# Layer 0's gates made with tanh and dealt out over the slots, and the next image's context started later

## The chip, the cores and the metric

The kernel runs on one core of a Trainium2 chip. The metric is the device time of one execution in microseconds (us); the number given for a kernel is the median of its runs. For the kernel before, three runs took 9255.66, 9257.32 and 9263.38 us, so the median is 9257.32 us.

The engines are named as in the profile: PE multiplies matrices (PEld is its weight load, which runs beside it), DVE is the vector engine, ACT the scalar engine that evaluates functions such as exp, POOL the general engine, SP the engine whose queue issues most of the DMA transfers. Each engine works through its own instructions in order.

## What is computed

Two layers are applied to eight images of 128 x 128 pixels with 128 channels. The change lies in layer 0 and in one part of layer 1 that layer 0's loop computes in advance. Cut to what matters:

```python
# layer 0: linear attention, per image; x is (pixels, 128)
q, k, v = split(x @ w_qkv, 3)                  # 4 heads of 32 channels
q = softmax(q, over the 32 channels of a head) * 32 ** -0.5
k = softmax(k, over all pixels of the image)
context = k^T v                                # 32 x 32 per head
o = (q context) @ w_out + b_out
x1 = layernorm(o) * gamma + beta + x
# layer 1: a selective scan; of it only the gate concerns us
xz = x1 @ Win
xb, z = split(xz, 2)                           # 256 channels each
...                                            # convolution, four scans, their sum y
out = layernorm(y * silu(z)) @ Wout
```

Here silu(z) = z * sigmoid(z), which also equals (z/2) * (1 + tanh(z/2)).

## The kernel before, in words

`layer0` keeps two whole images in on-chip memory, `xs[0]` and `xs[1]`, each a tile of 128 channels (partitions) by W = 128 columns by H = 128 rows in float32. Images are taken in the order ORDER = (0, 1, 4, 5, 2, 3, 6, 7); "image 3" below means the fourth of them. An image is worked on in NG = 32 groups of 512 pixels (GW = 4 columns). Every matmul of layer 0 is float32, and the program issues each as two passes.

Two pipelines of stages run over the groups.

- The **context** of an image (function `context`): `key` multiplies group g with the key weights (tile pk, L180) and ACT copies it out (k, L182). `larger` keeps a running maximum on DVE (L190, L192, and every fourth group L196, L197). `fold` and `spread` turn it into a new bound every fourth group (L206 to L221). `value` makes the values (pv, L225; copied by ACT, L226). `subtract` (DVE, L231) and `raise_to` (ACT exp, L234) make the exponentials, and `add` multiplies them with the values into the sum pc (L240).
- The **attention** of an image (function `attend`): `query` makes pq (L268), its maximum qm (DVE, L270) and the difference q (DVE, L272). `exponent` is the exponential (ACT, L275). `normalize` sums it (qs, L280), inverts it (L281) and scales q on POOL (L282). `through_wo` makes pg (L288), which ACT copies to gt (L290). `through_context` makes po (L294), adds the bias into o (DVE, L296) and squares it (ACT sq, L298). `variance` reduces that (var, L302). `scale` makes the diagonal matrix d on POOL (L308 to L313). `turn` makes pt (L321), and `finish` scales it (ACT x1t, L325) and adds the input in place, on POOL (L327).

A third piece is the **gate** (`gate_group`, L147): silu of the second half of x1 @ Win, two matmuls pz per group (L161), ACT's Silu from PSUM into z (L163) and a store to the array zs in HBM (L165). For images 0 to 5 of the order, the group is first copied by DVE into a small tile v, from `xs` read across its columns (L152, a step of 512 bytes between elements). For images 0, 1, 4 and 5 that copy also goes to HBM as x1. Since v takes one row from every column, it can only be made once the whole image is finished.

What sets the order of the work: `in_order` ties every instruction to the one recorded ahead of it on the same engine, so that the order in which `image(b)` calls its stages is the order on each engine. `image(b)` runs the attention of image b and the context of image b + 1 side by side in slots t = 0 to 38 (LATER = 1 delays the context by one slot). In each slot the stages of different groups stand in a fixed sequence. After slot 0 of images 1 to 6, `gate(b - 1)` does all 32 gate groups of the previous image in one block, and then issues the load of image b + 1 into the buffer that has come free. In the last image the gates are dealt out: slots 0 to 31 hold one gate group of image 6 each, and slots 4 to 35 one of image 7.

Buffers: all results of PE but two share six PSUM banks (pool `l0p`, tag "ps"). The tiles z and k share seven buffers (tag "k"). The tile v has four.

Of the kernel before, what the change touches and what calls it, by code (L numbers as in the profile page):

```python
# [8 lines left out]
F32 = mybir.dt.float32  # L9
BF16 = mybir.dt.bfloat16  # L10
AF = mybir.ActivationFunctionType
ALU = mybir.AluOpType
# [4 lines left out]
P = 128  # L17
B = 8
# [3 lines left out]
NC2 = 2  # L22
R = 8
K = 4
GW = 4
GN = GW * H
NG = W // GW
BK = 4
ORDER = (0, 1, 4, 5, 2, 3, 6, 7)
LATER = 1  # L30
CH = 1024
CW = CH // H
NCH = L // CH
# [44 lines left out]
def layer0(ctx: ExitStack, tc, xT, w_qkv, w_out, b_out, gamma, beta, win, x1, zs):  # L78
# [12 lines left out]
    nc = tc.nc  # L91
    const = ctx.enter_context(tc.tile_pool(name="l0c", bufs=1))
    wp = ctx.enter_context(tc.tile_pool(name="l0w", bufs=2))
    sm = ctx.enter_context(tc.tile_pool(name="l0s", bufs=4))
    ps = ctx.enter_context(tc.tile_pool(name="l0p", bufs=6, space=PSUM))
# [10 lines left out]
    nc.sync.dma_start(wq, w_qkv)  # L106
    wz = const.tile([P, NC2 * P], F32, name="wz")
    nc.sync.dma_start(wz, win[:, NC2 * P :])
    wo = const.tile([P, P], F32, name="wo")
    nc.sync.dma_start(wo, w_out)  # L110
    bb = const.tile([P, GW, P], F32, name="bb")
# [13 lines left out]
    xs = [const.tile([P, W, H], F32, name=f"x{i}") for i in range(2)]  # L125
# [13 lines left out]
    def group(b, g):  # L139
        return xs[b % 2][:, g * GW : (g + 1) * GW, :]  # L140

    def load(b, pieces=range(8)):
        for i in pieces:
            s = slice(16 * i, 16 * i + 16)
            nc.sync.dma_start(xs[b % 2][:, s, :], xT[ORDER[b], :, s, :])

    def gate_group(b, g):  # L147

        v = group(b, g)
        if ORDER[b] % K < 2 or ORDER[b] < B // 2:  # L150
            t = wp.tile([P, GW, P], F32, name="v", bufs=4)
            nc.vector.tensor_copy(  # L152
                t, xs[b % 2].rearrange("p w h -> p h w")[:, g * GW : (g + 1) * GW, :]
            )
            if ORDER[b] < B // 2:
                nc.sync.dma_start(x1[ORDER[b]][:, g * GN : g * GN + GN], t.rearrange("p w h -> p (w h)"))
            if ORDER[b] % K < 2:
                v = t
        for c in range(NC2):
            pz = ps.tile([P, GW, P], F32, name="pz", tag="ps")  # L160
            nc.tensor.matmul(pz, wz[:, c * P : c * P + P], v, start=True, stop=True)  # L161
            z = wp.tile([P, GW, P], F32, name="z", tag="k", bufs=7)
            nc.scalar.activation(z, pz, AF.Silu)  # L163
            dst = zs[ORDER[b], c][:, g * GN : g * GN + GN]
            nc.sync.dma_start(dst, z.rearrange("p w h -> p (w h)"))  # L165

    def gate(b):

        for g in range(NG):
            gate_group(b, g)  # L170
        if b + 2 < B:
            load(b + 2)

    def context(b):

        ks, pks, ms, runs, scales = {}, {}, {}, {}, {}

        def key(g):
            pk = ps.tile([P, GW, P], F32, name="pk", tag="ps")
            nc.tensor.matmul(pk, wq[:, P : 2 * P], group(b, g), start=True, stop=True)  # L180
            ks[g] = k = wp.tile([P, GW, P], F32, name="k", tag="k", bufs=7)
            nc.scalar.copy(k, pk)  # L182
            pks[g] = pk

        def larger(g):
            pk = pks.pop(g)
            j, i = divmod(g, BK)
            if i == 1:
                runs[j] = run = wp.tile([P, GW, P], F32, name="run")
                nc.vector.tensor_tensor(run, pk, ks[g - 1], ALU.max)  # L190
            elif i > 1:
                nc.vector.tensor_tensor(runs[j], pk, runs[j], ALU.max)  # L192

            if i == BK - 1:
                run = runs[j]
                nc.vector.tensor_tensor(run[:, 0:2], run[:, 0:2], run[:, 2:4], ALU.max)  # L196
                nc.vector.tensor_tensor(run[:, 0], run[:, 0], run[:, 1], ALU.max)  # L197

        def fold(g):

            j, i = divmod(g, BK)
            if i < BK - 1:
                return
            run = runs.pop(j)
            turned = ps.tile([P, P], F32, name="pmt", tag="ps")
            nc.tensor.transpose(turned, run[:, 0, :], ident)  # L206
            ms[j] = m = sm.tile([P, 1], F32, name="m")
            nc.vector.tensor_reduce(m, turned, AX.X, ALU.max)
            if j:
                nc.vector.tensor_tensor(m, m, ms[j - 1], ALU.max)  # L210
                scales[j] = a = sm.tile([P, 1], F32, name="a")
                nc.vector.tensor_tensor(a, ms.pop(j - 1), m, ALU.subtract)
            runs[j] = dg = sm.tile([P, P], F32, name="dg", bufs=2)
            nc.vector.tensor_scalar(dg, ident, m, None, ALU.mult)

        def spread(g):
            j, i = divmod(g, BK)
            if i == BK - 1:
                nc.tensor.matmul(pm[:, j % 2, :], ones, runs.pop(j), start=True, stop=True)
                if j:  # L220
                    nc.scalar.activation(scales[j], scales[j], AF.Exp)  # L221

        def value(g):
            pv = ps.tile([P, GW, P], F32, name="pv", tag="ps")
            nc.tensor.matmul(pv, wq[:, 2 * P : 3 * P], group(b, g), start=True, stop=True)  # L225
            nc.scalar.copy(vts[g % 3][:, :, 0:P], pv)  # L226

        def subtract(g):

            mb = pm[:, g // BK % 2 : g // BK % 2 + 1, :]  # L230
            nc.vector.tensor_tensor(ks[g], ks[g], mb.to_broadcast([P, GW, P]), ALU.subtract)  # L231

        def raise_to(g):
            nc.scalar.activation(ks[g], ks[g], AF.Exp)  # L234

        def add(g):
            k = ks.pop(g)
            j, n = divmod(g, BK)
            for i in range(GW):
                nc.tensor.matmul(  # L240
                    pc, k[:, i, :], vts[g % 3][:, i, :],
                    start=(n == 0 and i == 0), stop=(n == BK - 1 and i == GW - 1),
                )
            if n < BK - 1:
                return
            if j:
                nc.vector.scalar_tensor_tensor(total, total, scales.pop(j), pc, ALU.mult, ALU.add)
            else:
                nc.vector.tensor_copy(total, pc)
            if g == NG - 1:  # L250
                rs = sm.tile([P, 1], F32, name="rs")
                nc.vector.reciprocal(rs, total[:, P : P + 1])
                for h in range(NH):
                    s = slice(HD * h, HD * h + HD)
                    nc.vector.tensor_scalar(
                        ctxs[b % 2][s, s], total[s, s], rs[s, :], HD**-0.5, ALU.mult, ALU.mult
                    )

        return key, larger, fold, spread, value, subtract, raise_to, add

    def attend(b):
# [69 lines left out]

        return query, exponent, normalize, through_wo, through_context, variance, scale, turn, finish

    def image(b):

        key = larger = fold = spread = value = subtract = raise_to = add = None
        query = exponent = normalize = through_wo = through_context = None
        variance = scale = turn = finish = None
        later = LATER if b >= 0 else 0
        if b + 1 < B:  # L340
            key, larger, fold, spread, value, subtract, raise_to, add = context(b + 1)
        if b >= 0:
            (query, exponent, normalize, through_wo, through_context, variance, scale, turn,
             finish) = attend(b)

        def at(stage, g):
            if stage is not None and 0 <= g < NG:
                stage(g)

        for t in range(later + NG + BK + 2):  # L350
            a = t - later
            at(scale, t - 2)
            at(finish, t - 3)
            at(query, t)
            if b == B - 1 and t < NG:
                gate_group(b - 1, t)
            at(through_wo, t - 1)
            if b == B - 1 and 4 <= t < NG + 4:
                gate_group(b, t - 4)
            at(exponent, t)  # L360
            at(subtract, a - BK - 1)
            at(raise_to, a - BK - 1)
            at(key, a)
            at(normalize, t)
            at(fold, a - 1)
            at(value, a - BK - 1)
            at(larger, a)
            at(through_context, t - 1)
            at(add, a - BK - 2)
            at(turn, t - 2)  # L370
            at(spread, a - 1)
            at(variance, t - 1)
            if t == 0 and 0 < b < B - 1:
                gate(b - 1)

    with in_order(tc):
        load(0)
        load(1)
        for b in range(-1, B):
            image(b)  # L380
# [889 lines left out]
```

## Time and profile before

| what | value |
|---|---|
| median of the three runs | 9257.32 us |
| the profiled execution, its own time | 9261.02 us |
| its span, first to last instruction | 9259.2 us |
| layer 0 (to about the first instruction of layer 1) | 0 to 2388 us |
| layer 1, front part, then scan part | 2388 to 4400, 4400 to 9259 us |

All readings are from the one profiled execution. Inside layer 0, the starts of the query's exponential (L275), of which there are 32 for each image, mark the images:

| stretch of the attention | starts at us | lasts us |
|---|---|---|
| context of image 0 alone | 0 | 112.7 |
| image 0 | 112.7 | 227.0 |
| image 1 | 339.7 | 297.8 |
| image 2 | 637.5 | 298.7 |
| image 3 | 936.2 | 288.2 |
| image 4 | 1224.4 | 286.0 |
| image 5 | 1510.4 | 296.5 |
| image 6 | 1806.9 | 296.2 |
| image 7 (the last) | 2103.1 | to 2388: 285 |

A line of a timeline gives the start in us, the length in us, the engine, the line of the kernel, the operation, what is written and read, and in brackets how long the engine had been idle before it and what it waited for. A line of groups gives the engine, the operation, its tiles and shapes and the count, then the busy time, the mean length of one in ns, and the idle time before them.

### The profile page before, as it was taken

The page shows a single profiled execution, that of the slowest core. Times are in us where ns is not written, and L with a number is a line of the kernel's source. Part 1 is how long each engine was busy: PE and PEld are TensorE (multiplying, and loading weights), DVE is VectorE, ACT ScalarE, POOL GpSimd, SP SyncE. Part 2 cuts the span into 40 slices and gives each one's busy share as a digit, 9 for nine tenths or more (in the row PEclk, how much of TensorE's full clock was granted, in tenths as well). Part 3 has the DMA queues.
Part 4 walks back from the last instruction along what each step waited for, and adds up shares of the span by engine and source line. Part 5 has one row for each costly group of instructions (what it writes and reads, how often), then busy time and mean ns, then how long its engine had stood idle before and what let it go on. Part 6 is the DMA issues. An engine that isn't in the chain of part 4 may idle for free. (4 is left out here: it accounts for less than half of the span.)

```text
span 9259.2 us, 91316 instructions
## 1 busy us (share of the span) xinstructions
PE 6337.5 (68%) x24512; PEld 3096.6 (33%) x24512; DVE 7992.0 (86%) x7953; ACT 7099.7 (77%) x8066; POOL 7316.5 (79%) x4684
## 2 busy tenths in 40 slices
PE   8899998988899999999434636446364463643636
PEld 5555555554333333333101304114031140311403
DVE  6667666774699999999799999999999999999996
ACT  5555555657789999999688887887878888888885
POOL 3446444554588988888599899998999989999897
PEclk9999999999999999999655757557575575755857
DMA  1322333123478789888758769587695876957767
GB/s 76 146 84 96 137 121 146 70 109 137 148 242 249 251 246 244 245 246 241 206 154 238 208 185 258 158 230 216 179 260 159 222 225 178 257 165 218 230 174 211
DMA packets 934769, 1750.66 MB, mean 189 GB/s; under 512 B 150228, under 2 KB 376148, under 8 KB 926064
## 3 DMA queue, kind: packets, MB, share of 16 engines
q1 hardware_dynamic: 873328, 1509.92, 49.4%
q0 software_dynamic: 60928, 234.90, 13.8%
q8 instruction: 200, 3.28, 0.1%
q14 instruction: 313, 2.56, 0.1%
HBM read 1052.36 MB, written 692.12 MB: 188 GB/s over the span
## 5 line engine op out<-in xcount | busy, mean ns | idle before, releaser
L951 POOL TENSOR_TENSOR h<-ubt,sp 128x1024 f32<-128x1024 f32 x1024 | 2422.4, 2399 | 348.4 <-ACT mv L1058 124.1
L934 PE MATMUL px<-rows,dtw 128*128 128x512 bf16 x2048 | 953.5, 565 | 2266.2 <-DVE y L1001 1084.5
L534 DVE SCALAR_TENSOR_TENSOR acc<-xb,cw,acc 128x1024 f32<-128x1024 f32 x1024 | 1320.3, 1289 | 133.7 <-ACT xb L502 89.9
L526 POOL TENSOR_TENSOR tap<-tap 128x1024 f32<-128x1024 f32 x512 | 1224.0, 2394 | 243.9 <-ACT tap L524 220.6
L938 ACT ACTIVATE sp<-px 128x1024 f32<-128x1024 f32 x1024 | 1047.3, 1024 | 435.4 <-PE px L934 418.1
L961 DVE TENSOR_TENSOR_SCAN h<-px,h 128x1024 f32<-128x1024 f32 x512 | 1177.3, 2331 | 31.7 <-ACT px L942 15.1
L934 PEld LDWEIGHTS <-dtw 128*128 128x128 bf16 x2048 | 169.1, 110 | 3089.1 <-issue 1022.7
L959 DVE TENSOR_TENSOR_SCAN h<-px,h 128x1024 f32<-128x1024 f32 x512 | 1177.9, 2330 | 21.4 <-POOL h L951 18.8
L1009 POOL TENSOR_TENSOR y<-y,h 128x512 f32<-128x512 f32 x768 | 1159.8, 1559 | 3.8 <-DVE h L982 3.8
L942 ACT ACTIVATE px<-sp,sa 128x1024 f32<-128x1024 f32 x1024 | 1110.4, 1109 | 6.1
L515 PE MATMUL acc<-xi,wt 128*128 128x512 f32 x2048 | 938.3, 601 | 53.7 <-ACT ures L539 53.7
L524 ACT ACTIVATE tap<-xb,cw 128x1024 f32<-128x1024 f32 x768 | 837.3, 1139 | 15.2 <-POOL xb L499 15.1
L282 POOL TENSOR_TENSOR q<-q,qs 128x512 f32<-128x512 f32 x256 | 272.2, 1063 | 695.5 <-DVE qs L281 695.5
L938 ACT ACT_TABLE_LOAD x512 | 656.9, 1283 | 170.0 <-PE px L934 168.0
L942 ACT ACT_TABLE_LOAD x512 | 656.9, 1283 | 9.1
L1074 PEld LDWEIGHTS px<-wg,z 128*128 128x128 f32 x4096 | 575.3, 225 | 114.8 <-issue 109.1
L1074 PE MATMUL px<-wg,z 128*128 128x128 f32 x4096 | 574.7, 308 | 0.0
L967 PE MATMUL pc<-rows,csel 128*128 128x512 bf16 x1024 | 517.5, 586 | 78.2 <-DVE rstd L1062 74.5
L515 PEld LDWEIGHTS acc<-xi,wt 128*128 128x128 f32 x2048 | 375.1, 189 | 574.4 <-issue 411.9
L488 PE MATMUL pxb<-xi,wi 128*128 128x512 f32 x1024 | 496.2, 607 | 2.1 <-ACT xb L497 2.1
L298 ACT ACTIVATE sq<-o 128x512 f32<-128x512 f32 x256 | 161.2, 630 | 421.0 <-DVE o L296 419.8
L1001 DVE TENSOR_TENSOR y<-y,px 128x1024 f32<-128x1024 f32 x384 | 468.6, 1220 | 14.4
(153 smaller groups left out, 15038.8 us busy)
## 6 DMA issues: line engine op xcount, KB each, us to landing
ubt<-ubs SPq DMA_DIRECT2D x1024, 512.0 KB
zs<-z SPq DMA_DIRECT2D x512, 256.0 KB
ubs<-ures SPq DMA_DIRECT2D x256, 512.0 KB
ubs<-turned SPq DMA_DIRECT2D x256, 512.0 KB
z<-zs SPq DMA_DIRECT2D x256, 512.0 KB
y<-gs POOLq DMA_DIRECT2D x128, 1024.0 KB, 10.3
gs<-du POOLq DMA_DIRECT2D x96, 1024.0 KB, 8.6
rows<-xps SPq DMA_DIRECT2D x1536, 60.0 KB
```

Source lines behind the costliest of these rows:

```text
L515: nc.tensor.matmul(acc[:, s, :], wt[:, j, c, :], x, start=(j == 0), stop=(j == len(ON_PE) - 1))
L524: nc.scalar.activation(t, at(n, c, *d), AF.Copy, scale=weight(n, c, *d))
L526: nc.gpsimd.tensor_tensor(sums[n, c], sums[n, c], t, ALU.add)
L534: nc.vector.scalar_tensor_tensor(acc, at(n, c, *d), weight(n, c, *d), acc, ALU.mult, ALU.add)
L934: nc.tensor.matmul(p[:, hf * 512 : hf * 512 + 512], sl.dw[:, c * P : c * P + P], src, start=True, stop=True)
L938: nc.scalar.activation(t, da[n, c], AF.Softplus)
L942: nc.scalar.activation(da[n, c], sp[n, c], AF.Exp, scale=sa[:, sl.s, c : c + 1])
L951: nc.gpsimd.tensor_tensor(h, u, t, ALU.mult)
L959: nc.vector.tensor_tensor_scan(e[:, ::-1], x[:, ::-1], e[:, ::-1], start, ALU.mult, ALU.add)
L961: nc.vector.tensor_tensor_scan(e, x, e, start, ALU.mult, ALU.add)
L1009: nc.gpsimd.tensor_tensor(v[:, c], v[:, c], h[:, c], ALU.add)
L1074: nc.tensor.matmul(po[:, w, :], z[:, c, w * H : w * H + H], wg[:, c, :], start=(c == 0), stop=(c == NC2 - 1))
```

## The change

1. **Gates with tanh.** The gate weights wz are halved once at the start. `gate_tanh` takes tanh of pz on ACT into z. `gate_store` makes (z + 1) * pz on DVE in one scalar_tensor_tensor and stores it. The bank pz is held until that is done.
2. **The copy v** (`ready`) moves from DVE to ACT, and is issued at the end of the slot ahead of the one whose gate uses it.
3. **The gates are dealt out.** `plan` gives every slot up to two gate groups. From slot 0 of image b, two groups of image b - 1 per slot until they are used up, and then the load of image b + 1. From slot 35, when the attention of image b is through, one group of image b itself per slot. The context of image b + 1 starts LEAD = 2 slots after the last gate of image b - 1. By these rules the contexts that run beside images 0 to 6 start at slot 1, 16, 9, 12, 11, 11 and 11 (`laters`), and these images have 39, 54, 47, 50, 49, 49 and 49 slots. The gates done in an image's own late slots are 4, 19, 12, 15, 14, 14 and 14. Image 7 has 37 slots: one gate in slots 0 to 4, two in slots 5 to 17, one from slot 18.
4. **Order inside a slot.** The exponential of the query (`exponent`) is now recorded ahead of `through_wo`, so ACT does it before the copy gt; it was the other way round. The gate's pieces stand between the stages as the diff shows.
5. **Buffers.** z has four of its own; k keeps seven.

```diff
--- before.py
+++ after.py
@@ -27,7 +27,7 @@
 NG = W // GW
 BK = 4
 ORDER = (0, 1, 4, 5, 2, 3, 6, 7)
-LATER = 1
+LEAD = 2
 CH = 1024
 CW = CH // H
 NCH = L // CH
@@ -106,6 +106,7 @@
     nc.sync.dma_start(wq, w_qkv)
     wz = const.tile([P, NC2 * P], F32, name="wz")
     nc.sync.dma_start(wz, win[:, NC2 * P :])
+    nc.vector.tensor_scalar(wz, wz, 0.5, None, ALU.mult)
     wo = const.tile([P, P], F32, name="wo")
     nc.sync.dma_start(wo, w_out)
     bb = const.tile([P, GW, P], F32, name="bb")
@@ -144,32 +145,35 @@
             s = slice(16 * i, 16 * i + 16)
             nc.sync.dma_start(xs[b % 2][:, s, :], xT[ORDER[b], :, s, :])
 
-    def gate_group(b, g):
+    vs, pzs, zts = {}, {}, {}
+
+    def ready(b, g):
 
         v = group(b, g)
         if ORDER[b] % K < 2 or ORDER[b] < B // 2:
             t = wp.tile([P, GW, P], F32, name="v", bufs=4)
-            nc.vector.tensor_copy(
-                t, xs[b % 2].rearrange("p w h -> p h w")[:, g * GW : (g + 1) * GW, :]
-            )
+            nc.scalar.copy(t, xs[b % 2].rearrange("p w h -> p h w")[:, g * GW : (g + 1) * GW, :])
             if ORDER[b] < B // 2:
                 nc.sync.dma_start(x1[ORDER[b]][:, g * GN : g * GN + GN], t.rearrange("p w h -> p (w h)"))
             if ORDER[b] % K < 2:
                 v = t
+        vs[b, g] = v
+
+    def gate_project(b, g):
+        v = vs.pop((b, g))
         for c in range(NC2):
-            pz = ps.tile([P, GW, P], F32, name="pz", tag="ps")
+            pzs[b, g, c] = pz = ps.tile([P, GW, P], F32, name="pz", tag="ps")
             nc.tensor.matmul(pz, wz[:, c * P : c * P + P], v, start=True, stop=True)
-            z = wp.tile([P, GW, P], F32, name="z", tag="k", bufs=7)
-            nc.scalar.activation(z, pz, AF.Silu)
-            dst = zs[ORDER[b], c][:, g * GN : g * GN + GN]
-            nc.sync.dma_start(dst, z.rearrange("p w h -> p (w h)"))
-
-    def gate(b):
-
-        for g in range(NG):
-            gate_group(b, g)
-        if b + 2 < B:
-            load(b + 2)
+
+    def gate_tanh(b, g, c):
+        zts[b, g, c] = z = wp.tile([P, GW, P], F32, name="z", bufs=4)
+        nc.scalar.activation(z, pzs[b, g, c], AF.Tanh)
+
+    def gate_store(b, g, c):
+
+        z = zts.pop((b, g, c))
+        nc.vector.scalar_tensor_tensor(z, z, 1.0, pzs.pop((b, g, c)), ALU.add, ALU.mult)
+        nc.sync.dma_start(zs[ORDER[b], c][:, g * GN : g * GN + GN], z.rearrange("p w h -> p (w h)"))
 
     def context(b):
 
@@ -178,7 +182,7 @@
         def key(g):
             pk = ps.tile([P, GW, P], F32, name="pk", tag="ps")
             nc.tensor.matmul(pk, wq[:, P : 2 * P], group(b, g), start=True, stop=True)
-            ks[g] = k = wp.tile([P, GW, P], F32, name="k", tag="k", bufs=7)
+            ks[g] = k = wp.tile([P, GW, P], F32, name="k", bufs=7)
             nc.scalar.copy(k, pk)
             pks[g] = pk
 
@@ -331,12 +335,36 @@
 
         return query, exponent, normalize, through_wo, through_context, variance, scale, turn, finish
 
+    plan, laters, loads = {}, {-1: 0}, {}
+    done = [0] * B
+    for b in range(-1, B):
+        left = NG - done[b - 1] if b > 0 else 0
+        if b >= 0:
+            laters[b] = -(-left // 2) + LEAD if left else 1
+        for t in range(laters[b] + NG + BK + 2 if b < B - 1 else NG + 5):
+            gates = plan[b, t] = []
+            for _ in range(2 if b < B - 1 else 1):
+                if b > 0 and done[b - 1] < NG:
+                    gates.append((b - 1, done[b - 1]))
+                    done[b - 1] += 1
+                    if done[b - 1] == NG and b + 1 < B:
+                        loads[b, t] = b + 1
+            if b < B - 1:
+                own = b >= 0 and not gates and t > NG + 2
+            else:
+                own = done[b] <= t - 5
+            if own and done[b] < NG:
+                gates.append((b, done[b]))
+                done[b] += 1
+    assert done == [NG] * B
+    times = list(plan)
+    then = dict(zip(times, times[1:]))
+
     def image(b):
 
         key = larger = fold = spread = value = subtract = raise_to = add = None
         query = exponent = normalize = through_wo = through_context = None
         variance = scale = turn = finish = None
-        later = LATER if b >= 0 else 0
         if b + 1 < B:
             key, larger, fold, spread, value, subtract, raise_to, add = context(b + 1)
         if b >= 0:
@@ -347,31 +375,46 @@
             if stage is not None and 0 <= g < NG:
                 stage(g)
 
-        for t in range(later + NG + BK + 2):
-            a = t - later
+        for t in (t for i, t in times if i == b):
+            a = t - laters[b]
+            first, second = (plan[b, t] + [None, None])[:2]
             at(scale, t - 2)
             at(finish, t - 3)
             at(query, t)
-            if b == B - 1 and t < NG:
-                gate_group(b - 1, t)
+            if first:
+                gate_project(*first)
+                gate_tanh(*first, 0)
+            at(exponent, t)
+            if first:
+                gate_tanh(*first, 1)
+                gate_store(*first, 0)
             at(through_wo, t - 1)
-            if b == B - 1 and 4 <= t < NG + 4:
-                gate_group(b, t - 4)
-            at(exponent, t)
+            if second:
+                gate_project(*second)
             at(subtract, a - BK - 1)
             at(raise_to, a - BK - 1)
             at(key, a)
             at(normalize, t)
+            if first:
+                gate_store(*first, 1)
+            if second:
+                for c in range(NC2):
+                    gate_tanh(*second, c)
             at(fold, a - 1)
             at(value, a - BK - 1)
             at(larger, a)
             at(through_context, t - 1)
+            if second:
+                for c in range(NC2):
+                    gate_store(*second, c)
             at(add, a - BK - 2)
             at(turn, t - 2)
             at(spread, a - 1)
             at(variance, t - 1)
-            if t == 0 and 0 < b < B - 1:
-                gate(b - 1)
+            for g in plan.get(then.get((b, t)), ()):
+                ready(*g)
+            if (b, t) in loads:
+                load(loads[b, t])
 
     with in_order(tc):
         load(0)
```

## The prediction

> **What bounds the kernel now.** I read the busy time by stretch first. Only layer 0, up to about 2388 us, is touched. Three stretches: one around the gate block after image 1's slot 0, one of attention beside context, one in the last image.
>
> ```profile
> core 0: us, PE busy (x) PEld busy (x) DVE busy (x) ACT busy (x) POOL busy (x), PEclk, DMA share, GB/s
> 339.00:407.00 68.00, 62.30 (x130) 24.03 (x131) 26.13 (x35) 40.16 (x66) 1.65 (x1) 0.95 0.90 341
> 407.00:637.00 230.00, 205.71 (x1047) 137.19 (x1045) 173.62 (x305) 131.15 (x231) 143.12 (x159) 0.98 0.12 46
> 2103.00:2388.00 285.00, 238.84 (x886) 126.27 (x884) 109.48 (x190) 224.19 (x318) 144.92 (x160) 0.98 0.38 144
> ```
>
> PE is the busiest everywhere, but pipelined matmuls overlap in the records, so I looked at one slot. This is the vector engine, from image 0:
>
> ```profile
> 258.14 0.68 DVE L270 TENSOR_REDUCE qm<-pq 128x16 f32<-128x512 f32 x1
> 258.93 0.69 DVE L272 TENSOR_TENSOR q<-pq,qm 128x512 f32<-128x512 f32 x1
> 259.53 0.68 DVE L231 TENSOR_TENSOR k<-k,pmx 128x512 f32<-128x512 f32 x1
> 260.31 0.69 DVE L280 TENSOR_REDUCE qs<-q 128x16 f32<-128x512 f32 x1
> ...
> 261.99 0.68 DVE L296 TENSOR_TENSOR o<-po,bb 128x512 f32<-128x512 f32 x1
> 263.43 0.69 DVE L302 TENSOR_REDUCE var<-sq 128x4 f32<-128x512 f32 x1 [0.76 <-ACT sq L298]
> ```
>
> q comes 5.88 us after q, and the chain that returns is DVE's own: q, wait for exp, qs, larger, o, wait for the square, var, qm, q. The two slots of four with extra maximum work take 7.4 and 7.0. So four slots take 26.2 us. The scalar engine in that slot has slack, and does gt ahead of the exponential, which waits for q:
>
> ```profile
> 258.80 0.59 ACT L290 COPY gt<-pg 128x512 f32<-128x512 f32 x1 [0.63 <-PE pg L288]
> 259.65 0.63 ACT L275 ACTIVATE q<-q 128x512 f32<-128x512 f32 x1 [0.27 <-DVE q L272]
> 260.25 0.63 ACT L234 ACTIVATE k<-k 128x512 f32<-128x512 f32 x1
> ...
> 262.76 0.63 ACT L298 ACTIVATE sq<-o 128x512 f32<-128x512 f32 x1 [0.93 <-DVE o L296]
> ```
>
> The last image repeats every 8.69 us, with two table loads in the chain from square to exp:
>
> ```profile
> 2222.22 0.63 ACT L298 ACTIVATE sq<-o 128x512 f32<-128x512 f32 x1 [1.58 <-DVE o L296]
> 2222.76 0.76 ACT L325 ACTIVATE x1t<-pt,gb 128x512 f32<-128x512 f32 x1
> 2223.54 1.28 ACT L163 ACT_TABLE_LOAD   x1
> 2224.84 1.08 ACT L163 ACTIVATE z<-pz 128x512 f32<-128x512 f32 x2
> ...
> 2227.41 1.28 ACT L275 ACT_TABLE_LOAD   x1
> 2228.70 0.63 ACT L275 ACTIVATE q<-q 128x512 f32<-128x512 f32 x1
> ```
>
> From the groups of the whole layer and the waits:
>
> ```profile
> PE pk L180 <- DMA x<-in_x: 67.4, 7, 15.4
> ```
>
> is the wait for the next image after each block (about 52 us without the first). For a copy like the one that moves to ACT, layer 1 has a row: 512 floats read with a step of 512 bytes.
>
> ```profile
> L606 ACT COPY turned<-ures x92: 1066/1087/1109, 2675.0 to 4393.2; 128x512 f32<-128x512 f32 x92
> ```
>
> **What the Trainium skill says.** "ScalarE: Activation LUTs", section "Table sets: the hidden batching unit": exp and tanh are in one set, so between them nothing is reloaded; no run here shows it yet, but the built program of the change has one load in layer 0, where the trace has 78. The same page, "What ACT_TABLE_LOAD costs", gives 1283 ns and as much again for a drain; the trace has 1283 ns, but the next function starts 1.30 us after the load's start, so I take 1.3. "Advanced Engine Details and Errata", "SBUF Cachelines": a read that meets a new 16-byte line with each element is penalised. The trace agrees: 1.09 us for the strided ACT copy against 0.57 to 0.63 for contiguous ones, and 0.77 for the DVE copy v.
>
> **The change part by part.** Pitches (start to start in a queue) from the timelines: a 512-column product on PE 0.86 to 0.89, end 1.02 after start, about 0.1 more after a wait; ACT 0.54 for exp and square, 0.47 to 0.49 from PSUM, 0.67 for x1t, 1.0 for the strided copy (1.09 to its end); DVE 0.61. (z + 1) * pz is not in the trace; the form of L534, 1289 ns for 1024, gives 0.69 for 512, bounded by 0.6 and 0.8. Tanh like Silu: 0.60, and it cannot gain, as the length is per element. Only closed chains count, because each engine is bound to its order.
>
> Attention beside context (A+C). The exponential now stands ahead of gt on ACT. gt feeds po, PE stands still at po, and the next pq is behind po, pc and pt. New chain: q 0.72, exp 0.54, gt 0.59, po 1.01, pc and pt 1.78, pq 1.02, qm 0.77 = 6.45 against 5.88. The 7.4 and 7.0 slots keep their own chain. Four slots: 27.3 instead of 26.2, so 6.83 a slot. The first five slots of a context lack pv and pc: 30.5 as before.
>
> Attention with two gates (A+2G). The two copies v stand behind the square on ACT, and the first gate product waits for the first copy, with pg, the second gate and po behind it on PE. Chain: o to sq 0.77, sq 0.54, copy 1.09, wait 0.05, five PE products 4.44, po 1.06 = 7.95. PE alone would need 6.95.
>
> Context with one gate (C+G). Closed through the copy again: copy 1.09, pz 1.10, tanh 0.63, store 0.64, subtract 0.69, raise 0.57, key and value copies 0.94 = 5.66; without the key copy, at the end, 5.2. PE alone: 4.45 and 3.5.
>
> Image with context delay L (images 1 to 6), from first exponential to the next image's: two starting slots 13.1; A+2G 7.95 (L-5); out of it 7.4; two slots of attention alone at 5.88; 30.5; 6.83 (26-L); from the last exponential over finish, POOL (17.2 in image 0 of the trace) and the copy to the first own gate 17.3; 5.66 (L-3); 5 x 5.2; last slot with the next query 5.9. Sum 232.8 + 6.78 L. The six L add up to 70, so 1871. Less 19, because image 6 needs no copies for its own gates, and 4 for two slots with only one gate: 1848. These images take 1763.4 now (2103.1 - 339.7): **+85 us**. In this the block (64 us each), the load waits (the load now has two slots of attention and more, some 13 us, against 8 us of waiting) and 12 table loads are gone.
>
> Image 0: 26 A+C slots at +0.28 are +7, four own gates at the end +12: **+19**.
>
> Image 7: no copies, no loads. One gate: exp, tanh, gt, po, o, sq, var, qm, q = 6.37. Two gates: PE, 7.05. 30 + 13 x 7.05 + 13 x 6.37 = 204.5 for the 31 steps that take 264.7 now: **-60**.
>
> Halving wz once costs under 0.5 us beside loads: nothing. The table load of layer 1's first Silu stays ahead of work that waits for DMA: nothing. Stores: four z buffers and four z in a slot. SP issues them in order behind the x1 store, which waits for POOL. I count their landing some 1 to 2 us ahead of the next tanh: nothing; if that cover is gone, about 1 us in 30 slots, +30. The x1 stores of the copies v go with them, 0.5 MB per slot of two, behind the z stores on SP; nothing near waits for them, as four tiles v last two slots.
>
> Sum: +85 + 19 - 60 = +44 on 9261.0 (the profiled run; span 9259.2) is 9305. The median is 3.7 lower: **9301**.
>
> **Rivals.**
> - *Engines' sums, not chains, set the slots* (faster). Then A+2G takes 7.05, C+G 4.55 and 3.6, A+C stays at 6.54: about -38, -93 and -38 from my sum, so 9132; half of it gives 9217. For it: PE is busiest in every stretch. Against it: the slot shown follows a chain and not PE's sum. It decides once A+2G falls below about 7.4 and C+G below 5.1.
> - *The copy on ACT costs what it costs on DVE*, 0.77: some 115 copies on the chain at -0.32 are -37, so 9264, no change. Layer 1's copies run while POOL reads the same tile, which may lengthen them; but they hardly vary (1066 to 1109).
> - *z stores come late* behind the x1 store: 9330.
> - *Tanh reloads tables after all*: excluded by the built program.
>
> **How the numbers follow.** A measurement can tell about 0.2% (18.5 us) from no change. Forecast 0.52 (own range 9276 to 9365: copy 1.0 to 1.1, DVE store 0.6 to 0.8, the handing over of each image within 5 us), late stores 0.08, cheap copy 0.13, engines' sums wholly or in part 0.27 (9130 to 9238). Slower 0.60, same 0.13, faster 0.27. The range runs from 9190, which leaves out about half of the last, to 9365.
>
> **What would show it.** In the profile after: v on ACT near 1.09 us and PE waiting at pz for it; exponentials 7.9 us apart in A+2G, 6.4 in plain A+C slots, 6.4 and 7.05 in image 7; gates in late slots every 5.7 us; no DMA wait before pk; layer 0 ending near 2432. I am wrong if v takes under 0.8 us, or if ACT isn't what PE waits for in slots with copies.

## The result, and the profile after

| kernel | median us | lowest to highest | ratio to before, 95% interval |
|---|---|---|---|
| before (6 runs) | 9256.99 | 9252.85 to 9264.19 | |
| changed (6 runs) | 9287.68 | 9281.18 to 9289.37 | 1.0032 [1.0021, 1.0043] |

The change makes the kernel slower by 30.7 us, or 0.3%. The forecast was 9301, so 44 slower, with a range of 9190 to 9365. The profiled execution of the changed kernel took 9287.93 us (span 9286.1). The busy times by stretch, for image 1, image 4 and the last image:

```profile
core 0: us, PE busy (x) PEld busy (x) DVE busy (x) ACT busy (x) POOL busy (x), PEclk, DMA share, GB/s
360.00:705.00 345.00, 297.22 (x1240) 174.47 (x1239) 225.46 (x403) 225.59 (x372) 144.20 (x160) 0.99 0.35 133
...
1316.00:1607.00 291.00, 263.88 (x1175) 159.98 (x1174) 207.35 (x370) 191.26 (x324) 143.88 (x160) 0.99 0.26 99
...
2179.00:2401.00 222.00, 200.44 (x834) 119.08 (x832) 170.69 (x289) 129.79 (x225) 143.69 (x160) 1.00 0.39 150
```

Image 1 now takes 344 us instead of 298, and PE stands idle for 48 of them. The last image takes 222 instead of 285: ACT's busy time there fell from 224 to 130. Layer 1's first instruction comes at 2401.5 us instead of 2388.2.

**A slot of attention beside context.** First ACT, then PE, then two lines of DVE, in image 0:

```profile
259.51 0.63 ACT L279 ACTIVATE q<-q 128x512 f32<-128x512 f32 x1 [1.38 <-DVE q L276]
260.05 0.57 ACT L294 COPY gt<-pg 128x512 f32<-128x512 f32 x1
...
266.00 0.63 ACT L279 ACTIVATE q<-q 128x512 f32<-128x512 f32 x1 [1.54 <-DVE q L276]
```

```profile
260.67 1.13 PE L298 MATMUL po<-gt,ctxn 128*128 128x512 f32 x2 [0.38 <-ACT gt L294]
261.63 1.05 PE L244 MATMUL pc<-vt,k 128*128 128x129 f32 x8
262.52 1.06 PE L325 MATMUL pt<-d,o 128*128 128x128 f32 x8
263.42 1.02 PE L272 MATMUL pq<-x,wq 128*128 128x512 f32 x2
```

```profile
264.48 0.69 DVE L274 TENSOR_REDUCE qm<-pq 128x16 f32<-128x512 f32 x1
265.27 0.69 DVE L276 TENSOR_TENSOR q<-pq,qm 128x512 f32<-128x512 f32 x1
```

Follow the times: exponential at 259.51, gt from 260.05 to 260.62, po at 260.67, pq at 263.42 to 264.44. On DVE qm then starts at 264.48 and q at 265.27, and the next exponential at 266.00. That is 6.49 us, and at no step is there more than about 0.1 us to spare. Before, ACT did gt first and the slot took 5.88.

**A slot of attention with two gates**, in image 1, PE and ACT:

```profile
395.43 1.98 PE L166 MATMUL pz<-v,wz 128*128 128x512 f32 x4 [0.71 <-ACT v L155]
397.25 1.05 PE L292 MATMUL pg<-wo,q 128*128 128x128 f32 x8
398.14 1.88 PE L166 MATMUL pz<-v,wz 128*128 128x512 f32 x4
399.86 1.02 PE L298 MATMUL po<-gt,ctxn 128*128 128x512 f32 x2
```

```profile
393.79 0.63 ACT L302 ACTIVATE sq<-o 128x512 f32<-128x512 f32 x1 [1.04 <-DVE o L300]
394.32 2.02 ACT L155 COPY v<-x 128x512 f32<-128x512 f32 x2
...
401.70 0.63 ACT L302 ACTIVATE sq<-o 128x512 f32<-128x512 f32 x1 [1.05 <-DVE o L300]
```

From square to square it is 7.91 us. In between, the first copy v ends near 395.4, PE starts the gate's products only then, and po, which leads to the next square, stands behind five products: four of the gates and pg.

**A late slot with one gate**, in image 1, ACT:

```profile
631.10 1.05 ACT L155 COPY v<-x 128x512 f32<-128x512 f32 x1
633.37 0.60 ACT L170 ACTIVATE z<-pz 128x512 f32<-128x512 f32 x1 [1.22 <-PE pz L166]
634.22 0.60 ACT L170 ACTIVATE z<-pz 128x512 f32<-128x512 f32 x1 [0.26 <-PE pz L166]
635.31 0.63 ACT L238 ACTIVATE k<-k 128x512 f32<-128x512 f32 x1 [0.49 <-DVE k L235]
635.85 0.57 ACT L186 COPY k<-pk 128x512 f32<-128x512 f32 x1
636.31 0.59 ACT L230 COPY vt<-pv 128x512 f32<-128x512 f32 x1
636.79 1.07 ACT L155 COPY v<-x 128x512 f32<-128x512 f32 x1
```

The copies are 5.7 us apart. ACT idles in this loop, and PE waits 1.1 us for v in each of the next slots; neither is full.

The last image has no table load any more. ACT in one of its one-gate slots, 6.37 us long:

```profile
2366.61 0.63 ACT L302 ACTIVATE sq<-o 128x512 f32<-128x512 f32 x1 [2.00 <-DVE o L300]
2367.15 0.76 ACT L329 ACTIVATE x1t<-pt,gb 128x512 f32<-128x512 f32 x1
2368.44 0.60 ACT L170 ACTIVATE z<-pz 128x512 f32<-128x512 f32 x1 [0.53 <-PE pz L166]
2369.39 0.63 ACT L279 ACTIVATE q<-q 128x512 f32<-128x512 f32 x1 [0.35 <-DVE q L276]
...
2372.98 0.63 ACT L302 ACTIVATE sq<-o 128x512 f32<-128x512 f32 x1 [2.00 <-DVE o L300]
```

Two more readings of layer 0: the waits for DMA (us in all, times, longest), and the row of the copy v (count, then shortest, median and longest in ns).

```profile
PE pk L184 <- DMA x<-in_x: 15.2, 1, 15.2
ACT z L170 <- DMA zs<-z: 6.7, 7, 1.8
```

```profile
L155 ACT COPY v<-x x192: 1042/1070/1121, 337.6 to 1947.2; 128x512 f32<-128x512 f32 x192
```

Only the first load is still waited for, and ACT waits less than 7 us for the four z buffers.

### The profile page after: what moved, and what is told of

It reads as the page before. It is cut to its first block, busy times and chain, and to the rows that moved or that the text cites. A ratio compares the mean times of both kernels' runs of the same rounds, so it can differ in the third digit from the quotient of the medians.

```text
span 9286.1 us, 92164 instructions
## 1 busy us (share of the span) xinstructions
PE 6287.3 (68%) x24350; PEld 3090.5 (33%) x24512; DVE 8120.8 (87%) x8274; ACT 7153.9 (77%) x8182; POOL 7313.0 (79%) x4684
## 5 line engine op out<-in xcount | busy, mean ns | idle before, releaser
L977 PE MATMUL px<-rows,dtw 128*128 128x512 bf16 x1893 | 911.7, 574 | 2307.8 <-DVE y L1044 1057.7
L175 DVE SCALAR_TENSOR_TENSOR z<-z,pz 128x512 f32<-128x512 f32 x512 | 343.0, 683 | 227.4 <-ACT z L170 226.9
L312 POOL TENSOR_SCALAR var<-var 128x4 f32<-128x4 f32 x256 | 49.4, 193 | 561.7 <-DVE var L306 561.7
```

The source lines that it names most:

```text
L977: nc.tensor.matmul(p[:, hf * 512 : hf * 512 + 512], sl.dw[:, c * P : c * P + P], src, start=True, stop=True)
```

## The experiments

Each ratio is to runs of the kernel before on the same chip. "Changed" stands for the kernel after the change, 9287.7 us.

| kernel | median us | ratio to before, 95% interval | start of layer 1 |
|---|---|---|---|
| e1, gt first | 9215.9 | 0.9954 [0.9941, 0.9966] | 2336.0 |
| e2, copies early | 9220.6 | 0.9957 [0.9945, 0.9970] | 2337.4 |
| e3, both | 9124.7 | 0.9852 [0.9837, 0.9867] | 2239.5 |
| e4, tanh in the block | 9629.6 | 1.0399 [1.0385, 1.0413] | 2752.0 |
| e5, the same, copy ahead | 9231.2 | 0.9974 [0.9963, 0.9984] | 2349.6 |
| e6, both, lead 1 | 9112.1 | 0.9844 [0.9830, 0.9857] | 2230.7 |
| e7, product without copy | 9200.0 | 0.9939 [0.9927, 0.9952] | 2314.1 |
| e8, Silu dealt out | 9627.1 | 1.0399 [1.0383, 1.0414] | 2755.1 |
| e9, both, lead 0 | 9140.8 | 0.9875 [0.9859, 0.9892] | 2260.2 |

### e1: gt first again

```diff
             at(query, t)
             if first:
                 gate_project(*first)
                 gate_tanh(*first, 0)
+            at(through_wo, t - 1)
             at(exponent, t)
...
-            at(through_wo, t - 1)
```

> The changed kernel with one order put back: in each slot ACT copies gt ahead of the query's exponential. Theory (closed chains through the order on ACT and PE): the 112 slots of attention beside context after the first five go from four slots in 27.15 us to 26.2, about -28 us, and the 16 one-gate slots of image 7 from 6.37 to about 5.9, -8: 9252 us. Rival (the swap is harmless, because ACT has idle time and the slot is set by sums of engine time): no change, 9288.

Measured: 9215.9, so 72 less than the changed kernel, twice the forecast. The slots went where they were expected, from 6.48, 6.48, 7.20, 6.99 to 5.89, 5.89, 7.39, 6.99. The rest came from slots that I had not counted: slots of attention alone fell from 5.88 to about 5.08, the first slots of each context from 5.88 to 5.65, in image 1 the slot after the last one with gates from 7.25 to 5.09, and the two-gate slots of images 5 and 6 from 7.22 to 7.00. Those of images 1 to 4 stayed (7.92 and 7.97): their chain over the copy is another one. One-gate slots of image 7 only fell to 6.21. The swap alone costs more than the whole loss of the change, so the rival is out.

### e2: the copies earlier in the slot

```diff
                 gate_store(*first, 0)
             at(through_wo, t - 1)
+            for g in plan.get(then.get((b, t)), ()):
+                ready(*g)
...
             at(variance, t - 1)
-            for g in plan.get(then.get((b, t)), ()):
-                ready(*g)
```

> The changed kernel with the strided copies v, the same in number and length and still on ACT, issued earlier in the slot: after the first gate's pieces and the copy gt, ahead of the exponential of the keys and of the square. Theory (the copy closes a chain over the gate's product on PE): two-gate slots of images 1 to 4 fall from 7.9 to about 7.0 (some 32 slots, -30 us), the late slots with one gate from 5.66 and 5.2 to about 4.5 and 3.5 (some 50, -64): 9193 us. Rival (the 192 x 1.07 us of ACT time are the cost, wherever they stand): no change, 9288. Rival (ACT is now late for the square or the keys): slower than 9288.

Measured: 9220.6, so 67 less, not 95. ACT's work is the same, so its amount is not what these 67 us were lost to. From the last exponential of image 1 to the next image it is 100 us instead of 124, as the late slots got shorter. But the two-gate slots stopped at 7.42, and those of images 5 and 6 rose from 7.22 to 7.42. ACT in such a slot of image 1:

```profile
392.59 0.63 ACT L279 ACTIVATE q<-q 128x512 f32<-128x512 f32 x1 [1.18 <-DVE q L276]
393.13 0.58 ACT L170 ACTIVATE z<-pz 128x512 f32<-128x512 f32 x1
393.60 0.58 ACT L294 COPY gt<-pg 128x512 f32<-128x512 f32 x1
394.07 2.11 ACT L155 COPY v<-x 128x512 f32<-128x512 f32 x2
396.09 1.07 ACT L170 ACTIVATE z<-pz 128x512 f32<-128x512 f32 x2
397.05 0.63 ACT L302 ACTIVATE sq<-o 128x512 f32<-128x512 f32 x1
...
400.02 0.63 ACT L279 ACTIVATE q<-q 128x512 f32<-128x512 f32 x1 [1.18 <-DVE q L276]
```

This is a new chain: exponential, tanh, gt, two copies, two tanh, square, and from there over DVE's var, qm and q to the next exponential at 400.02. ACT has no gap up to the square. The second rival was wrong for the sum, but it named this: ACT is now late for the square, and the slots of images 5 and 6 got longer.

### e3: both

Both edits together; `through_wo` stands ahead of `exponent`, and the copies follow the first gate's pieces.

> Both of the above edits in the changed kernel. Theory: the two chains lie in different slots, so the gains add: -36 and -95, about 9157 us, faster than both kernels. Rival (one stall hides the other): no better than the better of the two alone.

Measured: 9124.7, which is 163 below the changed kernel, more than the two alone added (72 + 67). Two-gate slots now come down to PE's sum, as e1 takes gt out of e2's new chain. PE in image 1:

```profile
401.58 1.02 PE L298 MATMUL po<-gt,ctxn 128*128 128x512 f32 x2
402.43 1.10 PE L325 MATMUL pt<-d,o 128*128 128x128 f32 x8
403.37 1.02 PE L272 MATMUL pq<-x,wq 128*128 128x512 f32 x2
404.23 1.88 PE L166 MATMUL pz<-v,wz 128*128 128x512 f32 x4
405.94 1.05 PE L292 MATMUL pg<-wo,q 128*128 128x128 f32 x8
406.83 1.88 PE L166 MATMUL pz<-v,wz 128*128 128x512 f32 x4
```

No brackets, no idle time: 6.95 us a slot. The chain over ACT and DVE, from one exponential (401.25) to the next (408.21), takes 6.96, so by the trace PE is not the only limit left. This kernel is faster than both others, by 1.5% than the one before.

### e4 and e5: tanh in the block

e4 is the kernel before with this alone (the diff is cut to the lines that matter):

```diff
+    nc.vector.tensor_scalar(wz, wz, 0.5, None, ALU.mult)
...
-            nc.scalar.activation(z, pz, AF.Silu)
+            nc.scalar.activation(z, pz, AF.Tanh)
+            nc.vector.scalar_tensor_tensor(z, z, 1.0, pz, ALU.add, ALU.mult)
```

> The kernel before with tanh alone: wz halved, tanh on ACT, (z + 1) * pz on DVE, everything else (gates in a block after slot 0, copy v on DVE, context one slot behind) as before. Theory (the tanh is the gain and the dealing out is the loss): image 7 falls from 8.7 us a slot to PE's sum of about 7.0, -49 us; twelve table loads at the six blocks are -15; the blocks gain nothing more, or lose up to 30 us in all, as DVE then has 2.0 us of work for each group beside 2.05 for the group: 9195 to 9225 us. Rival (the table loads were hidden): no change, 9257.

Measured: 9629.6, slower by 4%. Image 7 did fall to 6.94 a slot, but the first four blocks, whose products read v, took 171 to 174 us instead of 63 to 70. PE in such a block:

```profile
399.77 3.54 PE L162 MATMUL pz<-v,wz 128*128 128x512 f32 x4 [2.05 <-DVE v L153]
405.36 2.84 PE L162 MATMUL pz<-v,wz 128*128 128x512 f32 x4 [2.05 <-DVE v L153]
```

The next copy v stands on DVE behind this group's multiplications, which wait for tanh, which waits for the product, which waits for v. I had added up DVE's work and overlooked that it had become a closed chain of 5.4 us a group. PE is slow in it, too: the two products, 1.9 us in the dealt-out slots, take 2.7 to 3.6 us here, at a granted clock of 0.64 (345 to 505 us). e5 tests the reading by recording the next group's copy ahead (again cut):

```diff
+        if b < B - 2 and g + 1 < NG:
+            gate_copy(b, g + 1)
         for c in range(NC2):
```

> The kernel before with tanh in the block, as in the last run but with the copy v of the next group issued on DVE ahead of this group's two multiplications. Theory (the block of the last run closed a chain: v, product, tanh, multiplication, next v): the four blocks of images whose gates read v fall from 171 to 174 us back to 62 to 67, image 7 stays at 6.94 us a slot, and the twelve loads at the blocks are gone: 9190 to 9210 us, faster than before. Rival (tanh with its multiplication is too much for DVE in a block): blocks of 100 us and more, above 9400.

Measured: 9231.2. The chain is gone (blocks of 71 to 72 us, at a clock of 1.00 from 345 to 405 us), so the reading holds and the rival is out. These four blocks are not shorter than with Silu, and DVE has about 2.1 us of work per group in them: 0.73 for the copy and twice 0.69. I had expected 62 to 67, so the 9190 to 9210 were missed. Tanh with the gates left in their blocks is worth 0.3%. The last image gives more than that (230 us instead of 285); images 3 and 4 give some 19 us back.

### e6 and e9: how far the context must lag

Both have e3's orders; LEAD is 1 in e6 and 0 in e9.

> The changed kernel with both orders mended, and the next image's context one slot instead of two behind the last gate. Theory (a slot of lead costs 5.1 for a slot of attention alone and 4.2 for a late slot, against 6.5 for one of both): -2.7 us for each of six images, 9109 us against 9125, if the load still lands in time; it has then about 9 us. Rival (the load is late, as it was before the change): a wait for DMA ahead of pk of 3 us and more in each image, 9125 or slower.

> Both orders mended and no lead: the next context starts in the slot after the last gate of the image whose buffer it takes. Theory (the load needs about 9 us from its issue to the first piece, and only some 3 are left): pk waits for DMA about 5 us in each of six images, which more than eats the 2.7 us saved per slot: about 9125 us against 9112 with a lead of one. Rival (the load lands in time): 9100 or less.

Measured: 9112.1 and 9140.8. The waits of PE for the load, the first image left out, are these in e6 and then in e9:

```profile
PE pk L184 <- DMA x<-in_x: 1.1, 2, 0.6
```

```profile
PE pk L184 <- DMA x<-in_x: 28.0, 6, 5.2
```

So one slot of lead is enough and none is not: six waits of up to 5.2 us. e6's interval overlaps e3's, but its layer 0 ends 9 us earlier; its median is the lowest here. Both sizes were off. e6 gained 12.6 us on e3 and not 16. e9 came out 16 us above its forecast: the waits (28 us in all) are about those expected, but the second slot of lead saved next to nothing beside them, as layer 0 ends 29.5 us later than in e6. The load is also quicker than I had it: in e9 5.1 to 5.6 us pass from its issue on SP to the first product of the keys, and not 9, but that product is due within 1.4 us of the issue.

### e7: the product does not read the copy

```diff
-            if ORDER[b] % K < 2:
-                v = t
```

> The changed kernel with all copies v still made on ACT in the same place and stored to x1, but the gate products read the image's columns instead of v. This leaves out the turn of the gates of images 0, 1, 2 and 3, so zs holds their pixels in another order. Theory (the dependence of the product on the copy is the cost, not the copy's time on ACT): two-gate slots of images 1 to 4 fall from 7.93 to the 7.22 of images 5 and 6 (-22 us), and the late slots as in images 4 and 5 (78.7 us instead of 101.3 from the last exponential on in image 3), about -72 in all: 9194 us. Rival (ACT's time is the cost): 9288.

Measured: 9200.0, against 9194 expected. All 192 copies are still made, in the same places; only the gates' products do not wait for them. Two-gate slots fell from 7.92 to 7.22, and the stretch after the last exponential of image 1 from 124 to 101 us. In the changed kernel's order the dependence of the product on the copy costs 88 us; the same copies, when no product waits for them, are not what sets these slots. In e2's order their 2 us did stand in a chain, so this holds for the order and not for copies as such.

### e8: dealt out with Silu

The changed kernel without the halving of wz, with AF.Silu for AF.Tanh and without the multiplication in `gate_store`.

> The changed kernel with Silu in place of tanh: wz not halved, no multiplication on DVE, the gates dealt out in the same places. Its program has 364 table loads in layer 0. Theory (a load costs its 1.3 us only where ACT is on the chain: in two-gate slots and in image 7, and is hidden behind the wait for DVE and PE in the late slots): about 2 us in 47 two-gate slots, 2.3 in the 31 slots of image 7, 1 in the 92 late slots, about +260 on 9287: 9450 to 9600 us. Rival (all 363 added loads count): 9287 + 470 = 9757. Rival (ACT has room for them): 9287.

Measured: 9627.1, so 339 more for 363 loads, 0.93 us a load: above the 9450 to 9600 I gave, below the first rival's 9757. Two-gate slots of images 1 to 4 took 10.0 us as expected. But in late slots only half of the loads' time was hidden: from the last exponential of image 3 on it is 120 us instead of 101, so 1.3 us for each of 15 slots with two loads. And one-gate slots of image 7 took 10.24 us instead of 6.37, which is 3.87 more, while their two loads are 2.57. Most of the rest is po, in the changed kernel and then in e8:

```profile
2371.03 1.13 PE L298 MATMUL po<-gt,ctxn 128*128 128x512 f32 x2 [0.88 <-ACT gt L294]
```

```profile
2724.00 2.07 PE L297 MATMUL po<-gt,ctxn 128*128 128x512 f32 x2 [3.31 <-ACT gt L293]
```

The loads keep gt back, PE waits 3.3 us instead of 0.9, and po then takes 0.94 us longer. The granted clock in these slots is 0.83 (2660 to 2740 us), against 1.00 in the changed kernel's (2310 to 2390). So with Silu the gates dealt out in this order cost 4% against the kernel before. The Trainium skill's page "ScalarE: Activation LUTs", section "Table sets: the hidden batching unit", puts exp and tanh in one set, and the traces agree: one load in layer 0 with tanh, 364 with Silu.

## Why the prediction was right, step by step

In the profiled executions, from attention start to attention start, in us:

| image | forecast against before | measured |
|---|---|---|
| 0 | +19 | 248.1 - 227.1 = +21.0 |
| 1 to 3, by the forecast's formula | 341, 292, 314 | 344.2, 295.7, 315.5 |
| 4 to 6, by the formula | 305, 307, 288 | 291.3, 287.1, 284.9 |
| 1 to 6 | +85 | +55 |
| 7, to layer 1 | -60 | 222.0 - 285.1 = -63 |
| layer 0 | +44 | +13.3 |

**The chains held.** Attention beside context: 6.45 forecast (its terms as printed add up to 6.43), 6.48 measured. Two gates with a copy: 7.95 and 7.92. Late slots: 5.66 and 5.7. Image 7: 6.37 and 7.05, against 6.37 and 6.94. e1 and e2 opened the chains by order alone, e7 opened one by its data; this is shown, not only argued. The copy's price, 1.09 taken from layer 1, was 1.07.

**One term was mis-sized.** I let the copies of all of images 0 to 5 close the chain. For images 4 and 5 the copy only goes to x1 and the product reads the columns, so the late slots of these images, and the two-gate slots that do their gates (images 5 and 6), were overpriced: images 4, 5 and 6 came out 14, 20 and 3 us under the formula. The late part of images 4 and 5 took 78.7 us where that of image 3, with one slot more, took 101.3, and the two-gate slots of images 5 and 6 took 7.22 instead of 7.92. Against this, the first five slots of a context took 32.3 us in image 1 and 30.9 in images 2 to 6 where I had 30.5, as the swap on ACT costs there as well (in e1, which undoes it, they take 29.4), and the slot after the last one with gates took 7.25 us in most images instead of 5.88.

**Two things were not in the sum.** Layer 0 accounts for only 13 of the 27 us between the two profiled executions. By the first Silu of layer 1 the difference is 19.4. At the hand-over the last multiplication of the gates on DVE takes 5.75 us, behind a cast and beside POOL, which clears layer 1's buffers:

```profile
2403.13 5.89 DVE L464 CAST ident<-ident 128x128 bf16<-128x128 f32 x1
2403.27 5.75 DVE L175 SCALAR_TENSOR_TENSOR z<-z,pz 128x512 f32<-128x512 f32 x1
2403.89 4.43 POOL L496 MEMSET xb<- 128x5200 f32 x1
```

The last z store waits for it, and the first loads of layer 1 are queued behind that store on SP. From layer 1's start to its first Silu it is 31.0 us before and 37.2 here, and 36.2 to 37.4 in the other six kernels with tanh dealt out; but 32.0 and 32.2 in e5 and e4, where the last multiplication is over before POOL's long memset, and 30.8 in e8, which has none. So about 5 of the 6 us go with that multiplication, and about 1 with the table load of the first Silu, which e4 and e5 have too and which I had put at nothing. No run changed the hand-over alone. The other 7.5 us lie in the scan, which nothing touches; from its first to its last scan instruction the ten other traces differ from before by -4.6 to +8.8 us, the changed kernel by the latter. Why is open. So layer 0 gave 13 of the 44 us forecast for it, and the total of 31 came nearer only through what was not in the sum: that is luck, the chains are not.

**The rivals.** That the engines' sums set the slots is refuted for this order: in two-gate slots with a copy PE's sum of 6.95 was reached only with both orders mended (e3, e6, e9). That rival named what a better order gives, and e6 reached 9112, below the 9132 it named. The cheap copy is out (1.07 us). ACT waited 6.7 us in all for late stores. Tanh reloads nothing: one table load in layer 0.

## What to carry to other kernels

When the order on each engine is fixed, price a slot by the closed chains that run through the queues, not by the busiest engine's sum alone: an instruction that moves one place in a queue can close a new chain even where that engine is idle more than a third of the time, as ACT is in layer 0 here. What helped here: put a copy that feeds another engine ahead of the instructions that wait for that engine's results, and put the instruction whose result another engine is waiting for ahead of one that itself waits. Tanh and spreading the gates over the slots together paid 1.6% here (e6), of which tanh in the blocks gives 0.3% (e5), but only after both orders were mended; as first made they lost 0.3%. Whether the copy v had to leave DVE for this was not tried.

## What the hardware showed that I had not expected

- A DVE multiplication that took 0.69 us elsewhere took 5.75 at the hand-over, and the small cast ahead of it 5.89; both end at 2409.02, just after POOL's last memset (2408.94). Before, with no multiplication there, the same cast took 6.05. The Trainium skill's page "SBUF — State Buffer", section "🔬 SBUF: two separate sides", describes a pair of ports that DVE, in some of its instructions, and POOL (GpSimd there) share, and that one holds for a whole instruction while the other waits. The cast's length fits that; the multiplication reads one operand from PSUM and seems only to stand behind the cast. No run here was made to test it.
- A table load of 1.28 us cost 0.93 us on average in e8, although ACT stands idle for more than a third of layer 0 in the changed kernel: only part of the loads fell into a wait of ACT.
- PE ran at a lower granted clock where a chain made it wait long in every slot: 0.64 in e4's blocks (waits of 2.05 us) and 0.83 in e8's one-gate slots (3.3 us), against 1.00 in the late slots of the changed kernel (1.1 us; 590 to 700 us). The length of one wait does not decide it alone: in the late slots of e8 PE waits 2.0 us for v, in slots of 6.6 us and more, and the clock is 0.95 (615 to 750 us). What brings it down was not tried. There a longer chain cost more than the link added to it.
